# Nine of sixteen score tiles gathered by DMA instead of eight, gathered tiles scored earlier, and evictions moved behind the spread

## The chip, the cores and the metric

The kernel runs on one core of one Trainium2 chip. The metric is the device time of one execution in microseconds (us); lower is better. The median of three runs of the kernel before is 3519.69 us.

## The reference, cut to what matters

There are 64 graphs of 256 nodes with 256 features each (`x`), and one adjacency matrix `adj` (256 x 256, about 3% of the entries nonzero, the diagonal among them) shared by all graphs. Three message-passing layers (called L0, L1 and L3) and one attention layer (L2, between L1 and L3) follow each other. A message-passing layer, for one graph `h`:

```python
pre_u = h @ W1[:d];  pre_v = h @ W1[d:]
hidden = relu(pre_u[u] + pre_v[v] + b1)          # for each pair (u, v)
S = sigmoid(hidden @ W2 + b2)                    # one score for each pair
a = (S * A).T @ h                                # a[v] = sum over u of S[u,v] A[u,v] h[u]
m = (A.T @ h) * h
z = beta1 * h + beta2 * (a @ Wa + ba) + beta3 * (m @ Wm + bm)
```

The scores are wanted only where `A` is nonzero, so the kernel computes them for the edges alone, some two thousand of them, and not for all 65,536 pairs.

## The kernel before, in words

**Work.** Graphs are taken in pairs. Two streams, side a and side b, alternate: while the *heavy* part of a stage (the scores of one pair in one layer) runs for one stream, the *light* part (everything else) runs for the other. One round takes four graphs, two for each side, through three layers, in six stages; sixteen rounds make the kernel. Everything is unrolled, in one order for each engine, written out by generators: `beside` walks through the steps of the light part, and each step says how many score tiles are to be put beside it: a number, or a pair (p, f), for `next(made)` p times and `next(got)` f times. A scheduler below decides the last details of the order on each engine.

**Edges.** The edges are laid out once, in `edges`, in sixteen tiles of up to 128 edges, named (k, m, i): u is in half k of the 128 nodes of block m, v in quarter i of the 256 nodes. Edges that don't fit go to a tile `left`, the diagonal to `own`. For each tile the kernel must form pu[u] + pv[v] for its 128 edges and the two graphs of the pair, 128 rows of 512 numbers. There are two ways:

- A *matmul tile* (list `FAST`): one matmul (L697) multiplies `pick`, a matrix of zeros and ones, by `pre`, in which ACT has put 64 rows of pu and 64 rows of pv (`rows_u` and `rows_v`, L751 and L760). `made` does these.
- A *gathered tile* (list `FETCHED`): pu and pv are written to two tables in DRAM by SP (L630), in halves of 128 nodes, and POOL gathers rows with two indirect DMAs (L742): the first brings rows of table u into SBUF, the second adds rows of table v to them. `got` does their scores. The first four gathered tiles read only the first half of each table.

Before, eight tiles go each way. `FETCHES` is the order of the issues on POOL: sixteen for the gathered tiles and two for `left`, a *batch* of eighteen a stage. `issue_after` keeps all of them in program order, so one batch follows the other. Six of a batch are issued as soon as its first table half is there (`AHEAD`), the rest when the scores of the stage begin.

**Scores.** Whichever way a tile came, DVE makes its scores (L661): for each graph, relu, times the row of W2, summed into one column of `raw`. ACT turns columns into `val` by tanh (L681), DVE multiplies `val` by the edge weights into `rm` (L689), and TensorE spreads `rm` to the 256 x 256 matrix `sa` (`spread`, L787; DVE adds the result to `sa` at L789). This is done in two parts: EARLY holds the diagonal, `left` and the tiles of m = 0, LATE those of m = 1. `early` (L771, L775) starts `sa` from the diagonal and `left`. `spread` of LATE must wait for the last gathered tile of the stage, and it is the first thing that the light part of the next stage does (`after`).

**The light part.** `after` is `spread` and `finish`: `hb` (L326 or L330), a product with `sa` (L281) copied to `aT`, the products with Wm and Wa (L366, in the last layer L352), and the addition that gives `hT` (L369). In a stage after L1, `attention` comes next. `before` then makes pu and pv of the next layer (matmuls L625, the copy of pu on ACT L626, the addition of pv on DVE L627), issues the table writes, makes `own` (L636), and then `mixed`: the product of h with `adj` (L281), multiplied by hT into `mT` on DVE (L316). Four stages of a round have no attention and are short; two have it and are long.

**PSUM.** The pool `ps` has five buffers, `ga` (the matmul tiles) three.

Of the kernel before, what the change touches and what calls it, by code (L numbers as in the profile page):

```python
# [15 lines left out]
P = 128  # L16
# [16 lines left out]
FAST = [(0, 0, 2), (0, 0, 3)] + [(0, 1, i) for i in range(4)] + [(1, 0, 2), (1, 0, 3)]  # L33
FETCHED = [(k, 0, i) for k in range(2) for i in (0, 1)] + [(1, 1, i) for i in range(4)]
# [3 lines left out]
FETCHES += [(-1, 0), (2, 1), (4, 0), (3, 1), (5, 0), (-1, 1), (6, 0), (4, 1), (7, 0), (5, 1), (6, 1), (7, 1)]  # L38

AHEAD = 6  # L40

# [37 lines left out]
def adj_seq_kernel(ctx: ExitStack, tc: tile.TileContext, a: dict, out: bass.AP):  # L79
# [15 lines left out]
    mm = nc.tensor.matmul  # L95
# [170 lines left out]
    def stages(pools):  # L266
# [16 lines left out]
        def flip(o, src):  # L283

            for m in range(2):
                for c in range(2):
                    nc.tensor.transpose(o[:, m, blk(c)], src[:, c, blk(m)], ident)  # L287
# [22 lines left out]
        def mixed(st, l):  # L310

            mT = one.tile([P, 2, 2, N], FP, tag="mT" + st["side"], name="mT")
            for g in range(2):
                t = psum()
                product(t, st["h"][g], adj)
                nc.vector.tensor_tensor(mT[:, :, g, :], t, st["hT"][:, :, g, :], ALU.mult)  # L316
                yield 0
            st["mT"] = mT
# [16 lines left out]
        def finish(st, l):  # L335

            sa, mT = st["sa"], st["mT"]
            few_scores = l == GNN[1]
            hb = kept(st, l)
            aT = one.tile([P, 2, 2, N], FP, tag="aT", name="aT")  # L340
            for g in range(2):
# [3 lines left out]
                yield 0 if few_scores else 1  # L345
            if l == LAST:
                for g in range(2):
                    z = psum()
                    for m in range(2):
# [4 lines left out]
                        yield m * (1 + g), 1  # L354
# [7 lines left out]
            for m in range(2):  # L362
                z = psum()
                for j, (w, y) in enumerate(((wm[l], mT), (wa[l], aT))):
                    for c in range(2):
                        mm(out=z, lhsT=w[:, c, blk(m)], rhs=y[:, c], start=j == 0 and c == 0, stop=j == 1 and c == 1)  # L366
                    if j == 0:
                        yield 0
                nc.vector.tensor_tensor(hT[:, m], hb[:, m], z, ALU.add)  # L369
                yield m if few_scores else (2 * m, 1)  # L370
# [14 lines left out]
            if l == GNN[1]:  # L385
                for g in range(2):
                    turn(g)
                    yield 0
# [4 lines left out]
        def attention(st):  # L393
# [21 lines left out]
            for g in range(2):  # L415
# [12 lines left out]
                yield 2 - g  # L428
# [9 lines left out]
            for g in range(2):  # L438
# [4 lines left out]
                yield 1  # L443
# [17 lines left out]
    def few(stack):  # L461
# [26 lines left out]
        def edges():  # L488
# [62 lines left out]
            for k, m in ((0, 0), (1, 0), (1, 1), (0, 1)):  # L551
# [4 lines left out]
                    for i in range(4):  # L556
                        nc.tensor.transpose(t[:, i, :], pick[:, k, 4 * m + i, :], ident)
# [24 lines left out]
            for m in range(4):  # L582
                nc.tensor.transpose(t[:, m, :], picko[:, m, :], ident)
# [14 lines left out]

        def before(st, l):
# [5 lines left out]
            flat = lambda t: t.rearrange("p m g d -> p m (g d)")  # L605
# [4 lines left out]
            got = {LAST: (1, 0, 1, 1), GNN[1]: (1, 1, 1, 1), GNN[0]: (0, 0, 2, 1)}[l]  # L610
# [5 lines left out]
            own = one.tile([P, 2, 2, D], FP, tag="own", name="own")  # L616
            st["pu"], st["pv"], st["pre"], st["own"] = pu, pv, pre, own
            t = one.tile([P, FIRST, 2, D], FP, tag="fetched" + st["side"], name="fetched")
            st["fetched"] = [t[:, f] for f in range(FIRST)]
            for m, g in order:  # L620
# [15 lines left out]
                nc.vector.tensor_tensor(own[:, m, g, :], t[:, 0, :], pv[:, m, g, :], ALU.add)  # L636
                if g == 1:
                    if m == 0:
                        rows_u(st, 0, 2, 0, 0)
# [320 lines left out]
```

## Time and profile before

| | |
|---|---|
| median of the runs | 3519.69 us (3514.27 to 3521.29, three runs) |
| profiled execution | 3531.84 us |
| its span | 3529.9 us |
| granted TensorE clock, mean | 0.992 |
| instructions | 48385 |
| DMA queue of the gathers (q0) | 427.93 MB, 60.7% of 16 engines' span |
| DMA queue of SP (q1) | 154.96 MB, 12.7% |

The profile shows one execution. Busy time is given for each engine: PE is TensorE's matmuls, PEld its weight loads, DVE VectorE, ACT ScalarE, POOL GpSimd, SP SyncE. A row of a group has the line, the engine, the operation, output<-inputs, the number of instructions, the busy time, the mean of one in ns, and the idle time just before them with what ended most of it. In a timeline, a row has start, duration, engine, line and operation, and in brackets the idle time before it and what ended it. A matmul of 32-bit floats shows as two instructions (two passes). For a gather, the POOL row is the time of its issue; the transfer lands later.

### The profile page before, as it was taken

The numbers are of one execution on the slowest core, as the hardware profiler recorded it, in microseconds if no ns is written. First come the engines' busy times: TensorE is split into PE (matmuls) and PEld (weight loads), VectorE is DVE, ScalarE is ACT, GpSimd is POOL, SyncE is SP. The second block draws the span as 40 slices with busy tenths as digits, with TensorE's granted clock in tenths as the row PEclk, the third lists the DMA queues.
The fourth block names the chain that finished last, engine by engine and source line by source line (L and its number), as shares of the span: only waits on it lengthen the run. The fifth ranks groups of instructions, "written<-read, shape, count | busy, mean of one in ns | idle before, by whom it ended". The sixth has DMA issues, their size and how long they took to land.

```text
span 3529.9 us, 48385 instructions
## 1 busy us (share of the span) xinstructions
PE 3446.7 (98%) x14328; PEld 2106.0 (60%) x14328; DVE 2605.4 (74%) x10584; ACT 1599.5 (45%) x2929; POOL 2227.1 (63%) x1754
## 2 busy tenths in 40 slices
PE   6999999999999999999999999999999999999998
PEld 3566565656656566565666656556565665656655
DVE  5777686777867777777777777768677787777776
ACT  2444444444444444444545445444444444444452
POOL 3747667576665757667576675766757566675754
PEclk7999999999999999999999999999999999999999
DMA  5768777687777867778687776867768677786865
GB/s 148 163 141 192 155 178 168 160 182 155 182 157 170 176 146 188 150 181 181 145 191 161 178 172 151 188 153 185 163 162 179 150 187 157 176 177 146 192 150 114
DMA packets 274733, 587.25 MB, mean 166 GB/s; under 512 B 37024, under 2 KB 54304, under 8 KB 274464
## 3 DMA queue, kind: packets, MB, share of 16 engines
q0 software_dynamic: 190464, 427.93, 60.7%
q1 hardware_dynamic: 82416, 154.96, 12.7%
q8 instruction: 116, 1.90, 0.2%
q10 hardware_dynamic: 1584, 1.20, 0.1%
q14 instruction: 153, 1.25, 0.1%
HBM read 466.51 MB, written 117.44 MB: 165 GB/s over the span
## 4 chain that ended last, share of the span: by engine, by line
PE 72%; DVE 11%; DMA 5%; POOL 5%; issue 5%; ACT 2%; ACTq 0%; POOLq 0%; DVEq 0%
PE ga L697 14%; PE ps L281 13%; PE ps L625 13%; PE ps L366 10%; PE ps L352 5%; POOL fetched L742 4%; PE ps L787 4%; PE ps L448 3%; DVE junk L661 3%; PE ps L407 3%; DMA fetched<-tablev,ids_v 3%; DVE rm L689 3%; PE ps L287 2%; DVE sa L775 2%; PE ps L401 2%
## 5 line engine op out<-in xcount | busy, mean ns | idle before, releaser
L742 POOL DMA_INDIRECT fetched<-tablev,ids_v x768 | 1210.7, 1576 | 355.3 <-issue 232.6
L742 POOL DMA_INDIRECT fetched<-tableu,ids_u x768 | 764.8, 996 | 824.1 <-DMA tableu<-pu 594.0
L697 PE MATMUL ga<-pre,pick 128*128 128x512 f32 x1536 | 769.7, 605 | 11.7 <-DVE junk L661 8.4
L625 PE MATMUL ps<-L_gnn_w,hT 128*128 128x512 f32 x1536 | 695.5, 596 | 5.8 <-DMA hT<-in_xT_dram 5.8
L661 DVE SCALAR_TENSOR_TENSOR junk<-ga,L_gnn_w2row 128x256 f32<-128x256 f32 x1536 | 582.7, 418 | 134.6 <-PE ga L697 122.6
L661 DVE SCALAR_TENSOR_TENSOR junk<-fetched,L_gnn_w2row 128x256 f32<-128x256 f32 x1536 | 595.1, 417 | 35.1 <-DMA fetched<-tablev,ids_v 35.0
L760 ACT COPY pre<-pv 64x512 f32<-64x512 f32 x768 | 473.5, 616 | 108.8 <-DVE pv L627 86.7
L625 PEld LDWEIGHTS ps<-L_gnn_w,hT 128*128 128x128 f32 x1536 | 285.1, 191 | 334.7 <-issue 313.6
L751 ACT COPY pre<-pu 64x1024 f32<-64x1024 f32 x384 | 392.9, 1039 | 3.9
L369 DVE TENSOR_TENSOR hT<-hb,ps 128x512 f32<-128x512 f32 x128 | 88.0, 687 | 412.9 <-PE ps L366 412.9
L697 PEld LDWEIGHTS ga<-pre,pick 128*128 128x128 f32 x1536 | 274.7, 191 | 179.2 <-issue 122.4
L281 PE MATMUL ps<-adj,h 128*128 128x256 f32 x1536 | 358.7, 386 | 11.1 <-DVE own L636 8.0
L281 PE MATMUL ps<-sa,h 128*128 128x256 f32 x1536 | 362.4, 385 | 3.7 <-issue 2.9
L281 PEld LDWEIGHTS ps<-sa,h 128*128 128x128 f32 x1536 | 290.3, 192 | 109.0 <-issue 46.2
L626 ACT COPY pu<-ps 128x256 f32<-128x256 f32 x384 | 142.4, 371 | 466.9 <-PE ps L625 443.2
L281 PEld LDWEIGHTS ps<-adj,h 128*128 128x128 f32 x1536 | 283.4, 190 | 80.0 <-issue 36.8
L330 ACT ACTIVATE hb<-hT,L_gnn_zbias,scas 128x512 f32<-128x512 f32 x128 | 97.4, 807 | 450.3 <-DVE hT L369 356.7
L689 DVE TENSOR_TENSOR rm<-gva,val 128x256 f32<-128x256 f32 x768 | 279.0, 417 | 9.7 <-ACT val L682 7.2
L787 PEld LDWEIGHTS ps<-rm,gu 128*64 128x64 f32 x3072 | 172.4, 137 | 139.2 <-PE ps L281 55.4
L787 PE MATMUL ps<-rm,gu 128*64 128x128 f32 x3072 | 215.9, 280 | 30.9 <-DVE rm L689 29.4
L344 ACT COPY aT<-ps 128x512 f32<-128x512 f32 x192 | 112.6, 586 | 293.2 <-PE ps L281 250.3
L366 PE MATMUL ps<-mT,L_gnn_Wm 128*128 128x512 f32 x512 | 240.6, 592 | 0.0
(155 smaller groups left out, 4200.2 us busy)
## 6 DMA issues: line engine op xcount, KB each, us to landing
tableu<-pu SPq DMA_DIRECT2D x192, 256.0 KB
tablev<-pv SPq DMA_DIRECT2D x192, 256.0 KB
hT<-in_xT_dram SPq DMA_DIRECT2D x32, 512.0 KB
h<-in_x_dram SPq DMA_DIRECT2D x64, 256.0 KB
out_dram<-h SPq DMA_DIRECT2D x64, 256.0 KB
fetched<-tableu,ids_u POOLq DMA_INDIRECT x768
fetched<-tablev,ids_v POOLq DMA_INDIRECT x768
L_gnn_w<-in_L_gnn_W_dram SPq DMA_DIRECT2D x6, 256.0 KB
```

The costliest lines, as they stand in the source:

```text
L281: mm(out=o[:, m, :], lhsT=lhs[:, c, blk(m)], rhs=rhs[:, c, :], start=c == 0, stop=c == 1)
L352: mm(out=z[:, m, :], lhsT=y[:, c, g, blk(m)], rhs=w[:, c, :], start=j == 0 and c == 0, stop=j == 1 and c == 1)
L366: mm(out=z, lhsT=w[:, c, blk(m)], rhs=y[:, c], start=j == 0 and c == 0, stop=j == 1 and c == 1)
L625: mm(out=t, lhsT=hT[:, c, g, blk(m)], rhs=w1[l][:, c], start=c == 0, stop=c == 1)
L626: nc.scalar.copy(pu[:, m, g, :], t[:, 0, :])
L661: nc.vector.scalar_tensor_tensor(junk, t, 0.0, w2row[l], ALU.max, ALU.mult, accum_out=raw[:, i : i + 1])
L689: nc.vector.tensor_tensor(rm[:, k, ms, g, :], gva[:, k, ms, :], val[:, i : i + 4].unsqueeze(2).to_broadcast([P, 4, 64]), ALU.mult)
L697: mm(out=t, lhsT=pick[:, k, 4 * m + i, :], rhs=pre[:, n], start=True, stop=True)
L742: this = nc.gpsimd.indirect_dma_start(out=to, out_offset=None, in_=rows, in_offset=bass.IndirectOffsetOnAxis(ap=ids, axis=0), compute_op=( ...
L751: nc.scalar.copy(st["pre"][h, f : f + n], st["pu"][h, m].rearrange("p g d -> p (g d)").unsqueeze(1).to_broadcast([64, n, 2 * D]),)
L760: nc.scalar.copy(st["pre"][halves[1 - k], n], st["pv"][halves[i % 2], i // 2].rearrange("p g d -> p (g d)"))
L787: mm(out=t[h, :, quarter(i)], lhsT=gu[:, k, 4 * m + i, :], rhs=rm[:, k, 4 * m + i], start=True, stop=True)
```

## The change

Six things change together.

- `FETCHED` gets a ninth tile, (0, 1, 3), and `FAST` loses it. `FETCHES` gets two issues, (8, 0) and (8, 1), so a batch has twenty. `pre` has seven tiles instead of eight.
- `FAST` is ordered with the four tiles of m = 0 first, and `got` makes only four matmul tiles, not all, before EARLY is turned to `val`; `early` comes at once after that.
- The numbers of the steps change: how many matmul tiles and gathered tiles stand beside each step of the light part. For `finish` they come from a table, `STEPS`.
- `own` moves from `before` (from PSUM, four additions of 128x256) to `made` (from SBUF, two additions of 128x512).
- The multiplication of `mixed` into `mT` is put off (`later`) until the second addition to `sa` in `spread` has been issued.
- Matmul tiles are tied to the matmul issued just before them, by `issue_after(issued[-1])`; and `rows_u` and `rows_v` are called in another order.

```diff
-FAST = [(0, 0, 2), (0, 0, 3)] + [(0, 1, i) for i in range(4)] + [(1, 0, 2), (1, 0, 3)]
-FETCHED = [(k, 0, i) for k in range(2) for i in (0, 1)] + [(1, 1, i) for i in range(4)]
+FAST = [(k, 0, i) for k in range(2) for i in (2, 3)] + [(0, 1, i) for i in range(3)]
+FETCHED = [(k, 0, i) for k in range(2) for i in (0, 1)] + [(1, 1, i) for i in range(4)] + [(0, 1, 3)]
...
-FETCHES += [(-1, 0), (2, 1), (4, 0), (3, 1), (5, 0), (-1, 1), (6, 0), (4, 1), (7, 0), (5, 1), (6, 1), (7, 1)]
+FETCHES += [(-1, 0), (2, 1), (4, 0), (3, 1), (5, 0), (-1, 1), (6, 0), (4, 1), (7, 0), (5, 1), (8, 0), (6, 1), (7, 1), (8, 1)]
...
+STEPS = {
+    GNN[0]: [(1, 1), (1, 1), (0, 1), (0, 0), (0, 1), (2, 1)],
+    GNN[1]: [(0, 1), (0, 1), (0, 1), (1, 0), (0, 1), (1, 1), (0, 0), (0, 0)],
+    LAST: [(1, 1), (1, 1), (0, 1), (0, 1), (1, 0), (1, 1)],
+}
...
-        def mixed(st, l):
-            mT = one.tile([P, 2, 2, N], FP, tag="mT" + st["side"], name="mT")
+        def mixed(st, l, later=None):
+            st["mT"] = mT = one.tile([P, 2, 2, N], FP, tag="mT" + st["side"], name="mT")
...
-                nc.vector.tensor_tensor(mT[:, :, g, :], t, st["hT"][:, :, g, :], ALU.mult)
+                times = (mT[:, :, g, :], t, st["hT"][:, :, g, :], ALU.mult)
+                if later is None:
+                    nc.vector.tensor_tensor(*times)
+                else:
+                    later.append(times)
...
         def finish(st, l):
...
-                yield 0 if few_scores else 1
+                yield STEPS[l][g]
...
-                        yield m * (1 + g), 1
+                        yield STEPS[l][2 + 2 * g + m]
...
-                    if j == 0:
-                        yield 0
+                    if j == 0:
+                        yield STEPS[l][2 + 2 * m]
...
-                yield m if few_scores else (2 * m, 1)
+                yield STEPS[l][3 + 2 * m]
...
         def attention(st):
...
-                yield 2 - g
+                yield 1
...
-                yield 1
+                yield (0, 1) if g == 0 else 1
...
         def before(st, l):
...
-            got = {LAST: (1, 0, 1, 1), GNN[1]: (1, 1, 1, 1), GNN[0]: (0, 0, 2, 1)}[l]
+            got = {LAST: (1, 0, 0, 0), GNN[1]: (0, 1, 2, 1), GNN[0]: (1, 0, 1, 2)}[l]
...
-                nc.vector.tensor_tensor(own[:, m, g, :], t[:, 0, :], pv[:, m, g, :], ALU.add)
-                if g == 1:
-                    if m == 0:
-                        rows_u(st, 0, 2, 0, 0)
-                    rows_v(st, 2 - 2 * m, 2, 0)
+                if (m, g) == (0, 1):
+                    rows_u(st, 0, 2, 0, 0)
+                    rows_v(st, 4, 2, 0)
+                if (m, g) == (1, 1):
+                    rows_v(st, 0, 2, 0)
+                    rows_u(st, 2, 2, 1, 0)
+                    rows_v(st, 2, 2, 1)
...
-            yield from mixed(st, l)
+            yield from mixed(st, l, later if past else None)
...
             def made():
                 for n, (k, m, i) in enumerate(FAST):
                     t = ga.tile([P, 2, D], FP, tag="ga", name="ga")
-                    mm(out=t, lhsT=pick[:, k, 4 * m + i, :], rhs=pre[:, n], start=True, stop=True)
+                    with tc.issue_after(issued[-1]):
+                        mm(out=t, lhsT=pick[:, k, 4 * m + i, :], rhs=pre[:, n], start=True, stop=True)
                     tile_scores(t, k, m, i)
...
-                    if n < 2:
-                        both(own[:, n], DIAGONAL + 2 * n, DIAGONAL + 2 * n + 1)
+                    if n in (2, 3):
+                        m = n - 2
+                        nc.vector.tensor_tensor(*(flat(t)[:, m] for t in (own, st["pu"], st["pv"])), ALU.add)
+                        both(own[:, m], DIAGONAL + 2 * m, DIAGONAL + 2 * m + 1)
+                    count.append(n)
                     yield
...
                     if f == FIRST:
-                        for _ in made:
-                            yield
+                        while len(count) < 4:
+                            next(made)
                         rated(left, REST)
                         rated_all(EARLY, 0)
                         yield
+                        early(st)
+                        yield
                     tile_scores(fetched[f], *block)
-                    if f == FIRST + 1:
-                        early(st)
...
         def spread(st, l):
...
-                nc.vector.tensor_tensor(sa[:, m], sa[:, m], t, ALU.add)
+                it = nc.vector.tensor_tensor(sa[:, m], sa[:, m], t, ALU.add)
+            with tc.issue_after(it.ins):
+                while later:
+                    nc.vector.tensor_tensor(*later.pop(0))
```

## The prediction

> **What bounds the kernel now.** I read the page's engine and group rows first, then the timelines of POOL and PE over one round (four graphs, six stages, about 215 us, sixteen rounds), then the chain of waits in it.
>
> ```profile
> PE 3446.7 (98%) x14328; PEld 2106.0 (60%) x14328; DVE 2605.4 (74%) x10584; ACT 1599.5 (45%) x2929; POOL 2227.1 (63%) x1754
> ...
> L742 POOL DMA_INDIRECT fetched<-tableu,ids_u x768 | 764.8, 996 | 824.1 <-DMA tableu<-pu 594.0
> ```
>
> By these rows TensorE is the bound (98% busy) and POOL, which issues the gathers, has room. POOL waited 594.0 us for a table, 37 us a round. Where that idle time lies decides the case, so I read the first and last gather issue of four consecutive batches, B1 (scores of the LAST layer of side b), B2 and B3 (GNN[0]), B4 (GNN[1], side a). Columns: start, duration, the instruction, the idle time before it.
>
> ```profile
> 1329.27 1.00 POOL L742 DMA_INDIRECT fetched<-tableu,ids_u  x1 [13.88 <-DMA tableu<-pu]
> ...
> 1357.27 1.54 POOL L742 DMA_INDIRECT fetched<-tablev,ids_v  x1 [0.30 <-issue]
> 1359.12 0.99 POOL L742 DMA_INDIRECT fetched<-tableu,ids_u  x1 [0.30 <-issue]
> ...
> 1388.23 1.54 POOL L742 DMA_INDIRECT fetched<-tablev,ids_v  x1 [0.70 <-DMA fetched<-tableu,ids_u]
> 1390.07 0.98 POOL L742 DMA_INDIRECT fetched<-tableu,ids_u  x1 [0.30 <-issue]
> ...
> 1418.80 1.54 POOL L742 DMA_INDIRECT fetched<-tablev,ids_v  x1 [0.30 <-issue]
> 1423.10 0.98 POOL L742 DMA_INDIRECT fetched<-tableu,ids_u  x1 [2.75 <-DMA tableu<-pu]
> ...
> 1449.74 1.64 POOL L742 DMA_INDIRECT fetched<-tablev,ids_v  x1 [0.30 <-issue]
> ```
>
> B1, B2 and B3 follow each other without a gap (0.30 us is the gap inside a batch too); B4 had 2.75 us to spare. The idle time sits ahead of B1 (13.88), B5 and B6, the batches whose tables come out of the longer attention stages. The four short stages have no room on POOL. The result of each batch is needed by the second half of `spread` (L787):
>
> ```profile
> 1367.60 1.09 PE L787 MATMUL ps<-rm,gu 128*64 128x128 f32 x16
> ...
> 1398.85 1.09 PE L787 MATMUL ps<-rm,gu 128*64 128x128 f32 x16
> ...
> 1431.20 1.42 PE L787 MATMUL ps<-rm,gu 128*64 128x128 f32 x16 [1.31 <-DVE rm L689]
> ...
> 1464.05 1.42 PE L787 MATMUL ps<-rm,gu 128*64 128x128 f32 x16 [0.50 <-DVE rm L689]
> ```
>
> So TensorE used B1 to B4 at 1367.60, 1398.85, 1431.20 and 1464.05, and twice already waited. The chain of waits over 1329 to 1470 shows what lies between a gather and that use:
>
> ```profile
> 1416.89 6.11 DMA fetched<-tablev,ids_v
> 1423.56 1.34 DVE rm L689 x4
> 1426.23 1.56 DVE sa L775 x4
> 1427.79 1.03 DVE junk L661 x6
> ```
>
> A gather lands 6.11 us after its issue begins (the other rounds' rows lie between 5.2 and 6.6); then DVE works through scores, `rm` and, in this kernel, `sa` and `mT`, before TensorE goes on.
>
> **The change, part by part.**
>
> *One matmul tile less.* In the chain one tile is two passes, 0.86 us (its mean row, L697, is 605 ns a pass with overlap). Six stages a round: TensorE sheds 5.2 us a round, 82 us in all, if nothing else ends last.
>
> *One gathered tile more.* It is two POOL issues: 0.98 + 0.30 for u and 1.55 + 0.30 for v, 3.13 us a batch. Issues are in program order, so each batch passes its delay on to the next until POOL idles. Count from B1's first issue, whose table comes out of TensorE work that the change leaves about as it is. Last issue of B1: 1357.27 + 3.13 = 1360.40; of B2, two batches longer: 1388.23 + 6.26 = 1394.49; of B3: 1418.80 + 9.39 = 1428.19. B4 can begin at 1428.19 + 1.85 = 1430.04 instead of 1423.10, past its table; it ran 26.64 us to its last issue, takes 3.13 more, and about 1.5 more for the first v issue, which in back-to-back batches waits for a u gather in a full queue (1.77 and 2.32 in B2 and B3, 0.37 in B4): 1461.3.
>
> *Evictions later and scores sooner.* `mT` now stands behind the `sa` additions, and EARLY needs only four matmul tiles, so `rm`, `sa` and `mT` no longer lie between the last landing and `spread`. What is left, from the changed program's order on DVE: two scores 0.7; then `own` (about 0.6) under the tanh on ACT, 0.85 with its hops; four `rm` 1.34; a hop of 0.25. That is 3.1 for B2; 4.1 for B1, whose tail also holds three `hb` of 0.4; 3.6 for B3 and B4, which hold two `pv` additions. Holding the two products of `mixed` longer costs at most the 1.3 us of the two multiplications where the five PSUM buffers run out; TensorE is waiting for `rm` at that place anyway, so I take nothing.
>
> *The sum.* Landing 6.11 and tail added to each last issue, against the old use: B1 1370.6 (+3.0), B2 1403.7 (+4.9), B3 1437.9 (+6.7), B4 1471.0 (+7.0). TensorE alone would come earlier each time (from 1370.6 a short stage of 31 us less 0.9 ends at 1400.7, before 1403.7), so POOL decides all four. The shortest I can make it: landing 5.2, no extra v wait, tails of 2.5, gives 1467.5, +3.4. B5 starts late but its use is 40 us away: nothing. From B4's use to the next B1, TensorE has two matmul tiles less (13, not 15) and one group of EARLY products (1.06) that used to fall outside: -0.7. In the second attention stage the scores of tiles 0 to 3 now stand ahead of the `hT` addition: tile 3's v issue comes 14.25 us after the batch's first (1286.48 to 1300.73), plus landing 4.9 to 6.1 and 1.3 on DVE is 20.5 to 21.7, where TensorE wants `hT` after about 18.6. This costs 1.9 to 3.1; I take 1.9, as the queue is empty there. A round: 7.0 - 0.7 + 1.9 = +8.2 us, between +2.7 and +12.
>
> [...]
>
> *At no cost.* `own` becomes two additions of 128x512 instead of four of 128x256, about the same DVE time, and not on the path except in the tails counted. ACT copies one `pre` tile less (616 ns a stage) on an engine 45% busy. The ties between matmuls fix an order and add no wait for data. SP's DMAs keep their number and order. If ACT's cover went, `pre` would come 0.6 us later at most.
>
> Sixteen rounds at +8.2 are 131 us. The profiled execution took 3531.84 (span 3529.9), 12 above the median 3519.69 of the runs shown: 3531.84 + 131 = 3663, less the same 12 is 3651. I say 3650.
>
> **Rivals.**
>
> *TensorE stays the bound (faster).* The mechanism: POOL's 37 us of idle time a round exceed the 18.8 us added, and the shorter DVE tail lets TensorE bear the delay. For it: 98% busy, and before B3 and B4 TensorE waited 0.38 + 1.31 and 0.50 for DVE, which a shorter tail removes. Price: -82, with those waits -117: 3437 to 3403. Against it: the idle time stands ahead of B1, B5 and B6, where a table is missing, and none of it can be spent in B2 to B4. The point from which it decides: B4's use would have to come before 1464.05, that is, the four batches would need 7 us less than counted. Chance 0.11.
>
> *Even.* The delay at B4 is only about 5 us, and the tile shed elsewhere pays for it: 3520. It needs a queue shorter than even the lower bound. Chance 0.04.
>
> *DVE held by late gathers (slower still).* Scores set sooner wait in order in front of `pv`, `hT` and `h`. Behind them wait the tables, so the next batch, and TensorE. At +12 a round it is 192 us: 3712. For it: in the changed order pv of the second table half stands behind the score of tile 7 (a stage of GNN[0]) or tile 8 (GNN[1]). Against: the first four gathers read only the first half of a table, so the second half is wanted only 12 us into a batch. Chance 0.2.
>
> *The change does not do what it says.* Its program has twenty issues a batch on POOL instead of eighteen and seven matmul tiles instead of eight, so this is out.
>
> **How the numbers follow.** The forecast of POOL-bound short stages, some +2.7 to +12 a round, has 0.65, at 3650. With DVE held, slower has 0.85. Two tenths of a per cent, 7 us, is about what a measurement of this kernel tells from no change. The range goes from the lower bound (+2.7 a round is 43 us, 3563, widened a little for a stall of the old kernel that also goes) to just above the DVE rival: 3545 to 3725. That leaves out the faster and the even case, 0.15, and little above.
>
> **What would show it.** Right: POOL issues without a gap from B1 to B4, 33 us a batch; TensorE idle for some 2 to 4 us ahead of the second half of `spread` in each short stage, released by `rm`; PE's busy share down to about 92%; rounds of about 223 us; idle time on `tableu` below 594 us, some 20 to 25 a round. Wrong: rounds of 210 us with PE at 98%; landings well under 5 us; or TensorE's waits ending on `hT` or `pv` rather than `rm`, which would be the DVE rival.

## The result: 7.2% slower

The changed kernel takes 3771.94 us (median of 4 runs, 3767.80 to 3777.76) where the kernel before took 3519.93 beside it: a ratio of 1.072, 95% interval 1.0701 to 1.074. The direction was forecast, the size was not: +252 us against +131, and above the range's 3725. The kernel before ran at 3520 to 3539 us in the different measurements below, so kernels are compared by their ratios to it.

The page of the changed kernel, engine rows, chain by engine, and three groups (busy, mean ns, idle time before them with its releaser):

```profile
PE 3453.5 (92%) x14136; PEld 2110.5 (56%) x14136; DVE 2628.9 (70%) x10398; ACT 1515.2 (40%) x2833; POOL 2527.0 (67%) x1946
...
PE 31%; POOL 22%; DMA 16%; issue 14%; DVE 13%; ACT 4%; POOLq 0%; another core or an unknown queue 0%; ACTq 0%; DVEq 0%; SPq 0%
...
L767 POOL DMA_INDIRECT fetched<-tableu,ids_u x864 | 895.9, 1037 | 759.6 <-DMA tableu<-pu 496.0
L678 DVE SCALAR_TENSOR_TENSOR junk<-fetched,L_gnn_w2row 128x256 f32<-128x256 f32 x1728 | 671.4, 421 | 508.1 <-DMA fetched<-tablev,ids_v 504.5
L104 PE MATMUL ga<-pre,pick 128*128 128x512 f32 x1344 | 692.9, 614 | 92.8 <-ACT pre L785 72.1
```

TensorE fell from 98% busy to 92%, and the chain that ended last (72% TensorE before) now holds 38% of POOL and DMA. Two rows are not in the forecast's sum. VectorE stood 504.5 us waiting for gathered rows; in the kernel before that row had 35.0:

```profile
L661 DVE SCALAR_TENSOR_TENSOR junk<-fetched,L_gnn_w2row 128x256 f32<-128x256 f32 x1536 | 595.1, 417 | 35.1 <-DMA fetched<-tablev,ids_v 35.0
```

TensorE's matmul tiles waited 72.1 us for ScalarE's `pre`. And TensorE's busy time did not fall by the 82 us of the shed tile: it rose by 6.8.

POOL's timeline over the first four batches of a round, the same batches as in the prediction (start, duration, instruction, idle time before it):

```profile
1408.42 0.99 POOL L767 DMA_INDIRECT fetched<-tableu,ids_u  x1 [14.24 <-DMA tableu<-pu]
...
1439.31 1.53 POOL L767 DMA_INDIRECT fetched<-tablev,ids_v  x1 [0.69 <-DMA fetched<-tableu,ids_u]
1441.15 0.99 POOL L767 DMA_INDIRECT fetched<-tableu,ids_u  x1 [0.30 <-issue]
...
1474.30 1.53 POOL L767 DMA_INDIRECT fetched<-tablev,ids_v  x1 [1.10 <-DMA fetched<-tableu,ids_u]
1476.13 0.99 POOL L767 DMA_INDIRECT fetched<-tableu,ids_u  x1 [0.30 <-issue]
...
1508.72 1.53 POOL L767 DMA_INDIRECT fetched<-tablev,ids_v  x1 [0.31 <-issue]
1510.56 1.08 POOL L767 DMA_INDIRECT fetched<-tableu,ids_u  x1 [0.30 <-issue]
```

B1 to B4 follow each other with 0.30 us, as forecast: B4's 2.75 us of spare time is gone. TensorE's timeline at the second half of `spread`, where these batches are used (L104 and L107 are the helpers that now issue every matmul and transpose):

```profile
1448.57 1.33 PE L104 MATMUL ps<-rm,gu 128*64 128x128 f32 x16 [1.58 <-DVE rm L706]
...
1483.34 1.33 PE L104 MATMUL ps<-rm,gu 128*64 128x128 f32 x16 [1.59 <-DVE rm L706]
```

Counted from B1's first issue, the uses of B1 and B2 come at 40.15 and 74.92 us; the forecast's were 41.3 and 74.4. For B3 and B4 TensorE ran both halves without a stop, 1.97 us from 1519.17 and from 1552.02, so the second half came about 1 us in, at 111.7 and 144.6 (forecast 108.6 and 141.7); the waits lie earlier. The same timeline, just ahead of B3's use, and then VectorE's at the first of these waits:

```profile
1507.74 3.87 PE L104 MATMUL ps<-L_gnn_w,hT 128*128 128x512 f32 x8 [1.88 <-DVE pv L642]
...
1518.11 1.12 PE L104 MATMUL ga<-pre,pick 128*128 128x512 f32 x2 [2.03 <-ACT pre L785]
```

```profile
1506.57 0.42 DVE L678 SCALAR_TENSOR_TENSOR junk<-fetched,L_gnn_w2row 128x256 f32<-128x256 f32 x1 [2.56 <-DMA fetched<-tablev,ids_v]
...
1507.27 0.42 DVE L642 TENSOR_TENSOR pv<-ps,L_gnn_b1row 128x256 f32<-128x256 f32 x1
```

VectorE waited 2.56 us for a gather; `pv` stood behind that score; TensorE waited 1.88 us for `pv`. This is the mechanism of the rival "DVE held by late gathers", and it happens in a round in which POOL is the bound too.

The rounds, from the first issue of one batch to the first of the next (us, mean over 12 or 13 rounds in the middle of the run; other choices of rounds move a column by up to 0.3), with the kernels that the experiments below use:

| kernel | ratio to before | B1 | B2 | B3 | B4 | B5 | B6 | round |
|---|---|---|---|---|---|---|---|---|
| before | 1 | 29.64 | 31.03 | 32.37 | 34.09 | 45.08 | 42.94 | 215.2 |
| changed | 1.072 | 32.95 | 34.81 | 33.74 | 35.33 | 46.94 | 46.76 | 230.5 |
| e1, new order, eight tiles | 1.0304 | 30.24 | 32.07 | 34.56 | 32.50 | 46.80 | 46.15 | 222.3 |
| e2, old order, nine tiles | 1.0499 | 32.90 | 33.83 | 34.24 | 37.95 | 44.85 | 42.90 | 226.7 |
| e14, e1 with the old steps and EARLY | 1.0116 | 29.99 | 31.28 | 33.17 | 33.64 | 46.17 | 43.74 | 218.0 |
| e17, e14 with the old copies | 0.9987 | 29.91 | 31.37 | 33.21 | 32.74 | 44.56 | 43.08 | 214.9 |
| e9, e1 with the old copies | 1.0250 | 29.80 | 31.45 | 34.15 | 32.62 | 46.33 | 46.31 | 220.7 |

A round is 15.4 us longer, not 8.2: 9.7 in B1 to B4 (forecast 7.0) and 5.7 in B5 and B6 (forecast 1.2).

### The profile page after: what moved, and what is told of

It reads as the page before. It is cut to its first block, busy times and chain, and to the rows that moved or that the text cites. A ratio compares the mean times of both kernels' runs of the same rounds, so it can differ in the third digit from the quotient of the medians.

```text
span 3772.7 us, 47913 instructions
## 1 busy us (share of the span) xinstructions
PE 3453.5 (92%) x14136; PEld 2110.5 (56%) x14136; DVE 2628.9 (70%) x10398; ACT 1515.2 (40%) x2833; POOL 2527.0 (67%) x1946
## 3 DMA queue, kind: packets, MB, share of 16 engines
q1 hardware_dynamic: 82416, 154.96, 11.8%
## 4 chain that ended last, share of the span: by engine, by line
PE 31%; POOL 22%; DMA 16%; issue 14%; DVE 13%; ACT 4%; POOLq 0%; another core or an unknown queue 0%; ACTq 0%; DVEq 0%; SPq 0%
PE ps L104 23%; POOL fetched L767 19%; DMA fetched<-tablev,ids_v 11%; PE ga L104 6%; DVE junk L678 5%; PE ps L107 2%; DMA fetched<-tableu,ids_u 2%; POOL left L767 2%; DVE rm L706 2%; DMA left<-tableu,left_u 2%; ACT pre L785 1%; DVE mT L817 1%; DMA tableu<-pu 1%; ACT logits L427 1%; ACT f L424 1%
## 5 line engine op out<-in xcount | busy, mean ns | idle before, releaser
L767 POOL DMA_INDIRECT fetched<-tablev,ids_v x864 | 1377.7, 1595 | 364.9 <-issue 220.2
L767 POOL DMA_INDIRECT fetched<-tableu,ids_u x864 | 895.9, 1037 | 759.6 <-DMA tableu<-pu 496.0
L678 DVE SCALAR_TENSOR_TENSOR junk<-fetched,L_gnn_w2row 128x256 f32<-128x256 f32 x1728 | 671.4, 421 | 508.1 <-DMA fetched<-tablev,ids_v 504.5
L104 PE MATMUL ga<-pre,pick 128*128 128x512 f32 x1344 | 692.9, 614 | 92.8 <-ACT pre L785 72.1
L104 PE MATMUL ps<-L_gnn_w,hT 128*128 128x512 f32 x1536 | 718.9, 611 | 23.6 <-DVE pv L642 12.0
L678 DVE SCALAR_TENSOR_TENSOR junk<-ga,L_gnn_w2row 128x256 f32<-128x256 f32 x1344 | 512.5, 420 | 165.0 <-PE ga L104 153.6
L104 PEld LDWEIGHTS ps<-L_gnn_w,hT 128*128 128x128 f32 x1536 | 287.1, 195 | 370.3 <-issue 290.7
L785 ACT COPY pre<-pv 64x512 f32<-64x512 f32 x672 | 414.3, 616 | 145.0 <-DVE pv L642 101.1
L104 PEld LDWEIGHTS ga<-pre,pick 128*128 128x128 f32 x1344 | 241.0, 192 | 263.7 <-issue 146.7
L104 PE MATMUL ps<-adj,h 128*128 128x256 f32 x1536 | 350.6, 381 | 19.9 <-DVE sa L800 19.7
L104 PE MATMUL ps<-sa,h 128*128 128x256 f32 x1536 | 362.5, 382 | 2.5 <-DVE sa L814 2.4
L104 PEld LDWEIGHTS ps<-sa,h 128*128 128x128 f32 x1536 | 293.7, 192 | 113.5 <-issue 62.1
L776 ACT COPY pre<-pu 64x1024 f32<-64x1024 f32 (+1 forms) x384 | 352.8, 934 | 6.7
L104 PEld LDWEIGHTS ps<-adj,h 128*128 128x128 f32 x1536 | 291.6, 191 | 107.1 <-DVE sa L800 37.5
L104 PE MATMUL ps<-rm,gu 128*64 128x128 f32 x3072 | 218.4, 290 | 61.8 <-DVE rm L706 61.8
L104 PEld LDWEIGHTS ps<-rm,gu 128*64 128x64 f32 x3072 | 184.4, 144 | 146.6 <-issue 104.4
L698 ACT ACTIVATE val<-raw,L_gnn_halfb 128x21 f32<-128x21 f32 x192 | 59.3, 309 | 501.8 <-DVE junk L678 498.4
L104 PE MATMUL ps<-aT,L_gnn_Wa 128*128 128x512 f32 x512 | 240.6, 592 | 0.0
```

What stands on the lines that cost most here:

```text
L104: issued[:] = [nc.tensor.matmul(**k).ins]
L678: nc.vector.scalar_tensor_tensor(junk, t, 0.0, w2row[l], ALU.max, ALU.mult, accum_out=raw[:, i : i + 1])
L698: nc.scalar.activation(val[:, cols], raw[:, cols], AF.Tanh, bias=halfb2[l], scale=0.5)
L767: this = nc.gpsimd.indirect_dma_start(out=to, out_offset=None, in_=rows, in_offset=bass.IndirectOffsetOnAxis(ap=ids, axis=0), compute_op=( ...
L776: nc.scalar.copy(st["pre"][h, f : f + n], st["pu"][h, m].rearrange("p g d -> p (g d)").unsqueeze(1).to_broadcast([64, n, 2 * D]),)
L785: nc.scalar.copy(st["pre"][halves[1 - k], n], st["pv"][halves[i % 2], i // 2].rearrange("p g d -> p (g d)"))
```

## The experiments

**Which half of the change costs what.** e1 keeps the new order with eight gathered tiles; e2 keeps the old order and gathers nine. e3 and e4 take the ninth tile's issues out of the changed kernel.

e1, from the changed kernel:

```
-FAST = ... + [(0, 1, i) for i in range(3)]
+FAST = ... + [(0, 1, i) for i in range(4)]
-FETCHED = ... + [(0, 1, 3)]
-FETCHES += [..., (8, 0), (6, 1), (7, 1), (8, 1)]
+FETCHES += [..., (6, 1), (7, 1)]
...
```

The part left out (`...`), here and in e2, fits the number of rows copied to the number of matmul tiles.

> The changed order with eight gathered tiles: (0, 1, 3) goes back to the matmul tiles. Theory Q (the loss of 252 us comes from the two more issues a batch on a POOL queue that was full in the short stages): 3490 to 3530, the order alone costs nothing. Theory O (the loss comes from the new order, which puts DVE and ACT behind gathers that land late, whatever their number): 3600 or more.

Measured: 3643.21 us, 1.0304 [1.0287, 1.0321].

e2, from the kernel before:

```
-FAST = [(0, 0, 2), (0, 0, 3)] + [(0, 1, i) for i in range(4)] + ...
+FAST = [(0, 0, 2), (0, 0, 3)] + [(0, 1, i) for i in range(3)] + ...
+FETCHED = ... + [(0, 1, 3)]
+FETCHES += [..., (8, 0), (6, 1), (7, 1), (8, 1)]
...
```

> The order of before with nine gathered tiles and seven matmul tiles, nothing else. Theory Q: 3700 to 3800, as slow as the changed kernel or slower, since the old DVE tail behind the last landing is longer. Theory O: under 3600.

Measured: 3710.74 us, 1.0499 [1.0478, 1.052].

e3, from the changed kernel:

```
-FETCHES += [..., (8, 0), (6, 1), (7, 1), (8, 1)]
+FETCHES += [..., (6, 1), (7, 1)]
-tile_scores(fetched[f], *block)
+tile_scores(fetched[min(f, 7)], *block)
```

> The changed kernel without the two gathers of the ninth tile: its score reads tile 7 again, so one tile of sixteen holds another tile's scores. Seven matmul tiles on TensorE, eighteen issues on POOL. Theory Q: TensorE sheds 82 us and POOL bears nothing: 3420 to 3480. Theory O: 3600 or more, as the order is unchanged.

Measured: 3644.79 us, 1.0314 [1.0297, 1.0332].

e4 leaves out only the tile's second gather, `(8, 1)`.

> The changed kernel with the first gather of the ninth tile only (the rows of table v are not added for that tile). One more issue of 1.28 us a batch instead of two of 3.13 us together. Theory Q: about four tenths of the way from the kernel without the ninth tile's gathers to the changed kernel, 3550 to 3600. Theory O: within 30 us of that kernel without the ninth tile's gathers, since the number of gathers then matters little.

Measured: 3711.97 us, 1.05 [1.048, 1.052].

What follows. Neither theory holds alone: e1 and e3 come out as theory O says, e2 as theory Q says, and e4, half of the way from e3 to the changed kernel, is nearer to theory Q's four tenths. The new order alone costs 3.0%, the ninth tile alone 5.0%; together they cost 7.2%, a little less than the sum. e3 has one matmul tile less than e1 and is not faster: under the new order TensorE's shed tile gains nothing. The tile's `u` and `v` gather cost 1.9% and 2.2% (e3 to e4 to the changed kernel). So the surprise is the new order: the forecast had given it about 1.9 us a round, 30 us, and e1 shows 3.0%, 108 us.

**One part of the order undone at a time**, each from e1.

e5: `mT` is made where it was (`mixed(st, l)` without `later`).

> The changed order with eight gathered tiles (3643 us, 108 above before), but mT is multiplied at once, as before, not behind the additions to sa. Theory P (the two products of mixed held in PSUM, two of five buffers, stop TensorE): 3540 to 3580. Theory S (the step numbers put the scores of gathered tiles too early beside the light part, so DVE stands waiting in front of pv, hT and h): within 20 us of 3643.

Measured: 3652.14 us, 1.0324 [1.0302, 1.0346].

e6: the step numbers of before.

```
-    GNN[0]: [(1, 1), (1, 1), (0, 1), (0, 0), (0, 1), (2, 1)],
-    GNN[1]: [(0, 1), (0, 1), (0, 1), (1, 0), (0, 1), (1, 1), (0, 0), (0, 0)],
-    LAST: [(1, 1), (1, 1), (0, 1), (0, 1), (1, 0), (1, 1)],
+    GNN[0]: [1, 1, 0, (0, 1), 0, (2, 1)],
+    GNN[1]: [0, 0, 0, 0, 0, 1, 0, 0],
+    LAST: [1, 1, (0, 1), (1, 1), (0, 1), (2, 1)],
...
-            got = {LAST: (1, 0, 0, 0), GNN[1]: (0, 1, 2, 1), GNN[0]: (1, 0, 1, 2)}[l]
+            got = {LAST: (1, 0, 1, 1), GNN[1]: (1, 1, 1, 1), GNN[0]: (0, 0, 2, 1)}[l]
...
```

The steps of `attention` and those around `st["turn"]` in `before` go back too (`...`).

> The changed order with eight gathered tiles, but with the step numbers of before (finish, attention and before). Theory S: 3530 to 3570, most of the 108 us comes back. Theory P: within 20 us of 3643. Theory E (EARLY, now sooner, waits for the gather of left): within 20 us of 3643.

Measured: 3713.95 us, 1.0508 [1.0482, 1.0533].

e7: no tie between a matmul tile and the matmul before it (`nullcontext()` for `tc.issue_after(issued[-1])`).

> The changed order with eight gathered tiles, but without the tie of each matmul tile to the matmul before it. Theories S, P and E: within 15 us of 3643, as the tie adds no wait for data. If the tie keeps a matmul tile from filling a gap of TensorE: 3600 or less.

Measured: 3635.25 us, 1.0281 [1.0259, 1.0302].

e8: EARLY behind all matmul tiles, `early` behind the sixth gathered tile.

```
-                        while len(count) < 4:
-                            next(made)
+                        for _ in made:
+                            yield
...
-                        early(st)
-                        yield
...
+                    if f == FIRST + 1:
+                        early(st)
```

> The changed order with eight gathered tiles, but EARLY is turned to val after all matmul tiles and early comes after the sixth gathered tile, as before. Theory E: 3540 to 3590. Theory S: 3620 or more, since the scores of the gathered tiles keep their places beside the light part, or slower than 3643, since the tail behind the last landing grows.

Measured: 3669.07 us, 1.0376 [1.0351, 1.0401].

What follows. Every theory that one of these four is the cause fell. `mT` and the tie are not told from nothing (the intervals overlap e1's). The step numbers and EARLY's place make it worse when one of them goes back alone. In e6 the cost has another face: TensorE waits 127 us for ScalarE's `ro`, which EARLY's products need (30 in e1).

**ScalarE's copies.** In the new order the stage before copies the rows of the third and fourth matmul tile too, at `(m, g) == (1, 1)`: one copy of `pu` and two of `pv` (1.04 and 1.25 us, together 2.3 and not the 3.5 of the expectation below) that used to stand behind LATE's tanh now stand in front of it. e9 puts them back in e1:

```
                 if (m, g) == (1, 1):
                     rows_v(st, 0, 2, 0)
-                    rows_u(st, 2, 2, 1, 0)
-                    rows_v(st, 2, 2, 1)
...
-                    if n in (0, 1):
+                    if n < 3:
                         with tc.issue_after(past[-1]) if past else nullcontext():
-                            rows_u(st, 2 * n + 4, 2, 0, 1)
-                            if n:
-                                rows_v(st, 2 * n + 4, 2, 0)
+                            rows_u(st, 2 * n + 2, 2, int(n == 0), int(n > 0))
+                            if n != 1:
+                                rows_v(st, 2 * n + 2, 2, int(n == 0))
```

> The kernel with the new order and eight gathered tiles (3643), with the copies of the third and fourth matmul tile's rows taken out of the stage before and put behind LATE's tanh, where the kernel before has them (about 3.5 us of ScalarE's work a stage that no longer stands in front of that tanh). Theory A (ScalarE's queue: these copies hold up LATE's tanh, and with it rm and the spread): most of the 108 us come back, 3540 to 3580, and the waits of DVE's rm on ACT's val fall from about 200 us in all to under 80. Theory B (the scores of gathered tiles stand too early in DVE's queue and DVE waits for gathers, whoever copies what): 3640 within 15, and DVE's waits on gathers stay near 300 us.

Measured: 3623.15 us, 1.025 [1.0229, 1.0272]. This is in neither theory's range. DVE's `rm` waited 112.9 us for ACT's `val` (200.3 in e1), but DVE now waited 390.3 us for gathers (306.9 in e1).

e10 makes `own` in `before`, from PSUM, in four adds, as the kernel before does.

> The kernel with the new order and eight gathered tiles (3643), with own added up as before, from PSUM in the four steps that make pu and pv. Theory A (ScalarE's queue): 3643 within 15, or slower, since DVE's four adds stand again in front of the next step. Theory O (own's two adds of 128x512 stand in the scores' tail, where DVE is the last): up to 60 us faster, 3580 to 3610.

Measured: 3636.41 us, 1.0283 [1.0264, 1.0302].

e11 is e9, e10 and e7 together.

> Copies late, own soon, and no tie between a matmul tile and the matmul before it, together, in the new order with eight tiles. Theory A: 3530 to 3575 (A's gain and some 8 us of the tie). Theory B: 3625 to 3645, the tie alone.

Measured: 3623.32 us, 1.0244 [1.0225, 1.0263].

e12 puts only the new list and the new places of the copies into the kernel before:

```
-FAST = [(0, 0, 2), (0, 0, 3)] + [(0, 1, i) for i in range(4)] + [(1, 0, 2), (1, 0, 3)]
+FAST = [(k, 0, i) for k in range(2) for i in (2, 3)] + [(0, 1, i) for i in range(4)]
...
-                if g == 1:
-                    if m == 0:
-                        rows_u(st, 0, 2, 0, 0)
-                    rows_v(st, 2 - 2 * m, 2, 0)
+                if (m, g) == (0, 1):
+                    rows_u(st, 0, 2, 0, 0)
+                    rows_v(st, 4, 2, 0)
+                if (m, g) == (1, 1):
+                    rows_v(st, 0, 2, 0)
+                    rows_u(st, 2, 2, 1, 0)
+                    rows_v(st, 2, 2, 1)
...
```

The part left out takes the same three copies out of `made`.

> The kernel before (3535 on the chip of the last runs) with one part of the change alone: the new list of matmul tiles and the new places of the copies of their rows; own, mT, the steps, the place of EARLY and the order of the scores are as before. Theory A: slower by 60 to 110 us, 3595 to 3645, with rm waiting for val. Theory B: within 15 us of before, since the scores and their waits for gathers stand where they stood.

Measured: 3590.56 us, 1.0149 [1.013, 1.0168].

e13 is e12 with the copies behind the tanh (the edit of e9): the list alone.

> The kernel before (3537) with the new list of matmul tiles alone; its copies are back in the scores, behind LATE's tanh. Theory A (the place of the copies is what cost 54 us in e12): 3530 to 3550. Theory L (the list: with it the tiles that need pre from the other half come in another order): stays at 3580 to 3595.

Measured: 3539.17 us, 0.9999 [0.9983, 1.0015].

What follows. In the old order theory A holds, though e12 is 4 us under its range: the list costs nothing, the place of three copies costs 1.5%. ScalarE's timeline in e12 at EARLY and LATE (`val` of 21 and of 16 columns):

```profile
1437.93 0.31 ACT L684 ACTIVATE val<-raw,L_gnn_halfb 128x21 f32<-128x21 f32 x1
1438.27 1.04 ACT L754 COPY pre<-pu 64x1024 f32<-64x1024 f32 x1
1439.34 0.22 ACT L685 ACTIVATE val<-val 128x21 f32<-128x21 f32 x1
...
1442.76 2.54 ACT L763 COPY pre<-pv 64x512 f32<-64x512 f32 x4 [2.27 <-DVE pv L627]
1445.33 0.31 ACT L684 ACTIVATE val<-raw,L_gnn_halfb 128x16 f32<-128x16 f32 x1
```

and in e13 at LATE:

```profile
1455.84 1.25 ACT L761 COPY pre<-pv 64x512 f32<-64x512 f32 x2 [1.17 <-DVE pv L627]
1459.10 0.31 ACT L682 ACTIVATE val<-raw,L_gnn_halfb 128x16 f32<-128x16 f32 x1 [2.01 <-DVE junk L662]
```

In e13 ScalarE comes to the tanh before its scores are there (it waits 2.01 us for DVE). In e12 four copies end as it starts, and a fifth, of 1.04 us, stands between EARLY's tanh and its addition, in front of `ro`. The waits view (total us, times, longest us) of e13, then of e12, shows what TensorE waited for `ro`:

```profile
PE ps L772 <- ACT ro L685: 3.8, 2, 3.1
```

```profile
PE ps L774 <- ACT ro L687: 36.6, 33, 3.1
```

VectorE's `rm` waited 50.9 us for `val` (7.0 in e13), and TensorE 39.3 us for `rm` (29.6). TensorE's idle time, its span less its busy time, went from 86.2 us to 126.4. So the wait of TensorE that grew most is the one for `ro`. The three copies were moved together, and no run parts what the one ahead of `ro` costs from what the two ahead of LATE's tanh cost. In the new order (e9 against e1) the same undoing gives 0.5% only, while VectorE's waits for gathers grow.

**Steps and EARLY together, gathers, and what remains.** e14 is e1 with e6's and e8's edits both.

> The new order with eight tiles, with the step numbers and the place of EARLY and of early as in the kernel before, both together (each alone made it slower: 3714 and 3669 against 3643). Theory M (steps and EARLY are matched to each other, and the new pair costs some 50 us by itself): 3580 to 3605, near e12, which differs only in own, mT and the tie. Theory N (they don't matter as a pair): 3643 within 15.

Measured: 3580.19 us, 1.0116 [1.009, 1.0141].

e16 leaves the eighth tile's two gathers out of e1:

```
-FETCHES += [..., (6, 0), (4, 1), (7, 0), (5, 1), (6, 1), (7, 1)]
+FETCHES += [..., (6, 0), (4, 1), (5, 1), (6, 1)]
-tile_scores(fetched[f], *block)
+tile_scores(fetched[min(f, 6)], *block)
```

> The new order with eight gathered tiles (3643), less the two gathers of the eighth tile; its scores read the seventh tile's rows, so they wait for nothing new. Theory G (what the new order costs is waiting for gathers, DVE's 307 us of it): half or more of the 108 us come back, 3540 to 3590. Theory H (the cost is in the order on the engines themselves): 3630 to 3645.

Measured: 3600.97 us, 1.0169 [1.0146, 1.0193]; DVE's waits for gathers 178.1 us.

e17 is e14 with e9's edit of the copies.

> The kernel of e14 (eight tiles, steps and EARLY as before: 1.0116 of before), with the copies of the third and fourth matmul tile's rows put back behind LATE's tanh. What is left of the change is the list, own in the scores, mT put off and the tie. Theory A+M (copies and the pair are the whole): 3525 to 3550 where before is 3539. Theory R (own, mT or the tie cost some 40 us in the old order): 3575 within 10.

Measured: 3526.03 us, 0.9987 [0.9976, 0.9997].

e18 is e17 with e7's edit, no tie.

> The kernel of e17 without the tie between a matmul tile and the matmul before it. Theory A+M: 0 to 10 us under e17, so at or a little under the kernel before, since DVE has two adds of 128x512 in place of four of 128x256 there. Theory R: as e17 within 5 if it is own or mT that costs, at the kernel before if it is the tie.

Measured: 3522.92 us, 0.9974 [0.9963, 0.9984].

What follows. The copies' place, and the steps with EARLY's place, are the whole of the order's loss. With their ratios to the kernel before:

| eight tiles | copies behind LATE's tanh | copies ahead of it |
|---|---|---|
| old steps and EARLY | 0.9987 (e17) | 1.0116 (e14) |
| new steps and EARLY | 1.0250 (e9) | 1.0304 (e1) |

The new steps with the new EARLY cost 2.6% with the copies back and 1.9% with them ahead; the copies 1.3% and 0.5%. They overlap, which is why undoing one of them in e1 gave so little. The step numbers and EARLY's place are a matched pair: at the copies' new place the four corners are 1.0116 (both old, e14), 1.0508 (EARLY new), 1.0376 (steps new) and 1.0304 (both new).

By the table of rounds the pair costs 5.8 us a round (e9 against e17): 0.8 in B1 to B4, 1.8 in B5 and 3.2 in B6. Its mark in the waits view is VectorE waiting for gathers (total us, times, longest us), first in e17, then in e9, which differs from it in the pair alone:

```profile
DVE junk L676 <- DMA fetched<-tablev,ids_v: 39.6, 35, 4.1
```

```profile
DVE junk L676 <- DMA fetched<-tablev,ids_v: 390.3, 254, 5.1
PE ps L107 <- DVE hT L384: 30.8, 17, 2.4
```

VectorE's timeline of e9 in the second attention stage (batch B6) shows one such place, and TensorE's what it did there:

```profile
1542.28 0.42 DVE L676 SCALAR_TENSOR_TENSOR junk<-fetched,L_gnn_w2row 128x256 f32<-128x256 f32 x1 [4.67 <-DMA fetched<-tablev,ids_v]
...
1543.88 0.42 DVE L676 SCALAR_TENSOR_TENSOR junk<-fetched,L_gnn_w2row 128x256 f32<-128x256 f32 x1 [0.82 <-DMA fetched<-tablev,ids_v]
...
1547.24 0.68 DVE L384 TENSOR_TENSOR hT<-hb,ps 128x512 f32<-128x512 f32 x1
```

```profile
1547.98 0.98 PE L107 MATMUL ps<-ident,hT 128*128 128x128 f32 x7 [1.67 <-DVE hT L384]
```

The `hT` addition stands behind scores that waited 4.67 and 0.82 us, and TensorE waits 1.67 us for it; in e17 the longest wait of that helper for `hT` is 0.4 us. e16 tries the same from the other side: with two gathers fewer and nothing else moved, 1.35 of the 3.04% come back. That is under the half that theory G asked and more than theory H allowed, so waiting for gathers is a large part of the order's cost and not shown to be all of it. Of e1's 112 us of span over the kernel before, TensorE's idle time holds 72 (83.2 to 155.1) and its busy time 40 (3446.7 to 3486.4); what stretched the busy time is not followed here. e17 and e18 stand at and a little under the kernel before. e18 beats it by 0.26%, just past what a measurement of this kernel tells from no change; what is left in it of the change is the list, `own` in two additions, and `mT` put off.

**The ninth tile: issues or bytes?** e15 keeps both issues of the changed kernel and halves their bytes.

```
                    if f < FIRST:
                        rows = rows[blk(0)]
+                    if f == 8:
+                        to, rows = st["fetched"][f][:, 0, :], rows.rearrange("n (g d) -> (n g) d", g=2)
...
```

> The changed kernel (nine tiles, 3772), in which the two gathers of the ninth tile move half their bytes: the same 128 rows each, of 1 KB in place of 2 KB; the scores of the tile's second graph read the first graph's rows. POOL still makes two issues. Theory P (the price of the ninth tile is POOL's two issues of 128 rows): 3772 within 20. Theory Q (it is the bytes on the DMA engines): about half of the 130 us back, 3690 to 3720.

Measured: 3725.80 us, 1.0523 [1.0498, 1.0548]. By the ratios, 2.0 of the ninth tile's 4.2% (1.072 less e1's 1.0304) come back, nearly half; theory P, issues alone, falls (theory Q's range ends 6 us lower). The groups of e15 show how:

```profile
L775 POOL DMA_INDIRECT fetched<-tablev,ids_v x864 | 1369.3, 1585 | 324.4 <-issue 227.3
L775 POOL DMA_INDIRECT fetched<-tableu,ids_u x864 | 884.8, 1024 | 768.5 <-DMA tableu<-pu 507.3
```

These means (1585 and 1024 ns, 1595 and 1037 in the changed kernel) are of all tiles; the ninth tile's own 96 issues each way take 1568 and 1039 ns, and 1591 and 1049 in the changed kernel. So an issue takes as long as with 2 KB rows, and POOL's idle time on `tableu` stays about the same (507.3 us, 496.0 in the changed kernel). But B1 to B4 last 133.6 us together where the changed kernel has 136.8 and e1 129.4. So some 4 us a round stay with the issues and about 3 go with the transfers: v issues wait for the u rows they add to (141.1 us over the run in the changed kernel, 92.3 here).

## Why the prediction was wrong, step by step

- *POOL decides B1 to B4: right.* B4's last issue was forecast at 1461.3, 132.0 us after B1's first; in the round shown it came at 1541.71, 133.3 after. The ninth tile under the new order (e1 to the changed kernel) adds 7.5 us to B1 to B4 where 7.0 was summed. That the sizes are so near is in part luck: the price by issues of 3.13 us a batch stands for a cost that is only partly issues (e15), and in the old order the same tile adds 11.8 us to B1 to B4 (e2).
- *The tail from last issue to use: right for B1 and B2, short for B3 and B4.* There it was 11.4 and 11.3 us in place of 9.7, with `pv` and `pre` late on the way to B3's. The landing of 6.11 held: the chain of the changed kernel has 6.54 and 5.63 us for two of its `v` gathers. The 0.85 and the 0.25 us with hops in that tail were estimates of mine. At B2 `rm` began 1.21 us after the last score (1480.89 to 1482.10) and the second half of `spread` 1.24 us after that (1483.34), where 0.85 and 1.34 + 0.25 were counted.
- *At no cost: wrong, and the first failed step.* Of ScalarE I counted that it copies one `pre` tile less, not that three copies move up in its queue, one ahead of `ro` and two ahead of LATE's tanh. The sentence "`pre` would come 0.6 us later at most" looked at who waits for `pre`; in the runs the instructions behind the copies wait. e12 against e13 prices that at 1.5%, 53 us, in the old order; in the new one it is 0.5% (e1 against e9). The 0.6 us were wrong too: with nine tiles TensorE waited for `pre` 42 times and up to 2.8 us, 72.1 us in all (69.9 in e2, 4.5 or less in e1 and e9). The copies of the last matmul tiles stand behind the `val` of the stage before, which waits for its last gather; that this is the way the delay takes is argued and not tested. The rest held: `own`, the ties and, taken at nothing elsewhere in the prediction, `mT` move the time by no more than the intervals tell (e10, e7, e5).
- *Scores sooner: the second failed step.* I priced it in one place, the second attention stage, at +1.9 us a round, and took VectorE's waits for gathers elsewhere as a rival with a chance of 0.2. The new steps and EARLY cost 3.2 us in that stage's batch, B6, 1.8 in B5, which I had put at nothing, and 5.8 a round in all (e9 against e17). So the waits are not a rival. The ninth tile's delay falls in B1 to B4 (e2: +11.8 and -0.3 in B5 and B6), VectorE's mostly in B5 and B6 (e1: +2.2 and +4.9), and across these stages they add. With the old pair e14 has +1.9 in B5 and B6, and e17 -0.4. The sum had to hold both; it held the larger one and a little of the other, and the range's top was that rival alone.
- *-0.7 from B4's use to the next B1: wrong sign.* The ninth tile adds 0.75 us to B5 and B6 (e1 to the changed kernel; about 0.5 over all full rounds).
- *TensorE sheds 82 us: this gain did not reach the sum's other side.* Its groups do show it (769.7 to 692.9 us in the matmul tiles), yet busy time rose by 6.8. About 55 us of the difference is the granted clock by the account in the last section (some 58 us lost against 3); the rest is the busy time that e1, with all eight matmul tiles, has over the kernel before.
- *What would show it.* PE at 92%: right. Rounds of 223: 230.5. Idle on `tableu` 20 to 25 a round: 31 (496.0 in 16). TensorE idle 2 to 4 us ahead of every second half of `spread`: 1.6 in B1 and B2, next to none in B3 and B4; of the 314 us in its waits view (start and end of the run included) 72.1 end on `pre`, 61.8 on `rm`, 48.3 on `ro`, 36.3 on `hT`, 12.0 on `pv`. By the prediction's own last sentence `hT` and `pv` are the DVE rival, and they come near `rm`; `pre` and `ro`, which it did not name, hold 120.4 us together.

## What to carry to other kernels

When a copy or an eviction is moved, look at the instruction that now stands behind it in the same queue, not only at who reads the copy: three copies, 2.3 us of them, moved up in one queue cost 1.5% in the old order. An order that puts consumers sooner gained nothing here where what they consume landed late: in e9 two of VectorE's scores waited 4.67 and 0.82 us for gathers, the `hT` addition stood behind them, and TensorE waited 1.67 us for it. Two such delays in different stages can add (1.0304 and 1.0499 alone, 1.072 together here), so a rival whose mechanism does not exclude the forecast's belongs in the sum. Undo parts in pairs before calling them harmless: here single undoings gave at most 0.5% or made it worse, the steps and EARLY together gave 1.9%, and with the copies all of it.

## What the runs showed of the hardware

In the changed kernel TensorE paid twice for some of its waits. That kernel in windows of 1 us around a wait of 2.18 us (1432.74 to 1434.92); the columns are the length, the busy shares of PE, PEld, DVE, ACT and POOL with their instructions, then the granted clock, the DMA share and GB/s:

```profile
1433.00:1434.00 1.00, 0.00 (x0) 0.00 (x0) 0.70 (x3) 0.95 (x3) 0.69 (x2) 1.00 1.05 381
1434.00:1435.00 1.00, 0.08 (x2) 0.08 (x2) 1.00 (x4) 0.84 (x2) 0.92 (x1) 1.00 0.77 156
1435.00:1436.00 1.00, 1.00 (x8) 0.63 (x8) 1.00 (x6) 0.00 (x0) 0.78 (x1) 0.79 0.87 139
...
1438.00:1439.00 1.00, 1.00 (x2) 0.34 (x1) 1.00 (x5) 0.00 (x0) 0.62 (x1) 0.50 0.93 176
1439.00:1440.00 1.00, 1.00 (x4) 0.49 (x3) 1.00 (x5) 0.34 (x1) 0.69 (x1) 1.00 1.01 240
```

Here the clock is halved some 0.7 us after work comes back and stays so for 3.4 us (0.4 us of the window from 1435, then three whole ones), which is 1.7 us of full clock on top of the wait. The eight matmul passes of 128x512 that start in it, at 1436.32, take 5.01 us; eight such passes at 1420.52, with the clock at 1.00, take 3.60. In the changed kernel the clock was below full in the 4 us after 1 of 41 idle stretches of about 1.5 us (1.25 to 1.75), 12 of 36 of about 2.0, 15 of 26 of about 2.5, and all 7 of 2.75 and more. In 20-us windows from 200 to 3480 us this loses some 58 us of full clock, against 3 before, 9 in e1, 34 in e15 and 87 in e2. So of the ninth tile's 131 us of span (e1 3641.5 to 3772.7) some 49 are clock; TensorE's idle time grew by 164 (155.1 to 319.2) and its matmul tiles shrank by 83 (775.8 to 692.9), which leaves next to nothing. In the old order the clock holds up to 84 of e2's 178 us. This is an account from traces; no run separates the clock from the waits.
